# Layer 1's edge sums in two batches per group instead of four, and a reordered last group, in a two-layer graph attention kernel

## The chip, the cores and the metric

The kernel runs on one core of a Trainium2 chip. The metric is the device time of one execution in microseconds. Three executions of the kernel before took 2071.87, 2076.14 and 2081.02 us; their median is 2076.14 us. One more execution was recorded by the hardware profiler; it took 2070.48 us, and all views of the profile are of that one.

The engines are called PE (TensorE, matrix products; PEld is its loading of weights), DVE (VectorE), ACT (ScalarE), POOL (GpSimd) and SP (SyncE). Each works through its own queue of instructions strictly in the order in which the program lists them, and waits for the others by semaphores.

## The reference

A graph has 3125 nodes with 768 features and 53125 edges, sorted by the node they go to. Each edge has one of three relations. Two layers of relational graph attention are followed by a residual and a layer norm:

```python
def rgat_conv(x, W, q, k, b, src, dst, etype, heads, out_ch, n_nodes):
    xr = jnp.einsum('nd,rdf->rnf', x, W)
    oi = xr[etype, dst]
    oj = xr[etype, src]
    alpha = jax.nn.leaky_relu(oi @ q + oj @ k, NEG_SLOPE)
    m = jax.ops.segment_max(alpha, dst, num_segments=n_nodes)
    e = jnp.exp(alpha - m[dst])
    z = jax.ops.segment_sum(e, dst, num_segments=n_nodes)
    a = e / (z[dst] + EPS)
    msg = (a[:, :, None] * oj.reshape(-1, heads, out_ch)).reshape(-1, heads * out_ch)
    return jax.ops.segment_sum(msg, dst, num_segments=n_nodes) + b

h = jax.nn.elu(rgat_conv(x, W1, q1, k1, b1, ..., HEADS1, OUT1, n))   # 4 heads of 192
out = rgat_conv(h, W2, q2, k2, b2, ..., HEADS2, OUT2, n)             # 1 head of 768
return _layernorm(x + out, axis=-1)
```

So each layer has a dense part (every node's row times three 768 x 768 matrices) and an edge part (for every edge the row of its source under its relation is fetched, weighted, and added up at its target).

## The kernel before

**Groups, slots, rounds.** The sorted nodes are cut into NB = 25 groups of up to 128 nodes. A group's edges lie in SL = 17 slots of 128 edges each (the first group has SLF = 14). Since the edges are sorted, a slot's targets lie in one or two of the four 32-node windows of its group; `WINDOW` lists them. `ROUNDS` puts the slots into seven rounds such that the slots of one round have different windows: rounds 0 to 2 have three slots each, rounds 3 to 6 two. A slot's turn is its place when the rounds are read one after another.

**Three phases.** Phase 1 makes layer 1's table of rows for every node and relation, and the attention weights of layer 1's edges. Phase 2 (707 to about 1480 us of the profile) does two things woven together: the edge sums of layer 1 for one group, and the dense part of layer 2 for the group before it. Phase 3 does the edge part of layer 2, the residual and the layer norm. The order of the instructions is written out by hand: each phase is a loop over steps k, and lists of events tell which function is called at which step. No planner decides anything.

**Phase 2, in its steps.** At step k `gather(k)` has POOL fetch the rows of slot number k by an indirect DMA into one of 14 buffers (the nine `share` tiles and five `g` tiles); a buffer is free again when the sums of the slot 14 places earlier have read it. `high(k - 3)` has DVE write the slot's weight matrices `selp` (four heads, 32 or 64 columns; one tensor_scalar each, L857), into a pool of 9 buffers. `sums(k - 5)` (L861) issues PE's products of weights and rows (L878). Each has 32 output rows, one window, so products of one round that go to different windows lie in different quarters of the array. The sums don't go out slot by slot: `sums` returns without doing anything until a round is complete that closes a batch, and then issues all rounds of the batch, round by round and within a round head by head. The batches are rounds 0 and 1, 2 and 3, 4 and 5, and 6 alone; the last turns of these are the 6th, 11th, 15th and 17th slot of a group.

After a group's last sums come `e_y` (DVE divides by the weights' sum and adds the bias; L884 to L891), `e_x` (ACT's exponential, L897), `e_h` (DVE, L901 and L902), three steps after `e_y` `e_t` (PE's six transposes, L909), then `e_s` (ACT's copy of the result into `hT`, its high half, L916) and `e_s2` (DVE's difference, its low half, L922). From the sixth step after `e_y` on, `d_part` is called 18 times over 17 steps: six products of 128 x 128 weights each (L934; three per feature tile: high times wH, high times wL, low times wH), three calls for one half of one relation's rows. `d_row` copies each half out of `po` by ACT (L942), and SP stores finished rows into layer 2's table (L948). The last quarters of layer 2's weights for relation 2 are loaded by ACT's DMA queue at steps 14, 19, 23 and 26.

In a middle group PE's order is therefore: six transposes, 6 dense products, rounds 0 and 1, 36 dense products, rounds 2 and 3, 24 dense, rounds 4 and 5, 12 dense, round 6, 30 dense, and the next transposes.

**Phase 3, its end.** For each group: DVE's two scans (L1089, L1091) give the maxima, L1094 the exponents, `a_exp` (ACT, L1098) the exponential, `a_back` (PE, L1102) turns it, `a_put` (DVE, L1107) copies it to `p`, `high` (L1115) and `sums` (L1129) follow. Then `e_y`, `e_n` (mean and variance, L1172 to L1176), `e_sd` (ACT's square root, L1180), `e_low` (DVE's reciprocal and product, L1185 and L1187), `e_out` (ACT's scaling, L1192, and the store). Exponential and root need different function tables in ACT; the build puts an ACT_TABLE_LOAD ahead of each activation whose table isn't the one in place. In the steps of the loop `e_sd` of one group comes one step ahead of `a_exp` of the next, and `e_low` two steps ahead of `a_put`.

Of the kernel before, what the change touches and what calls it, by code (L numbers as in the profile page):

```python
# [8 lines left out]
F32 = mybir.dt.float32  # L9
# [4 lines left out]
AF = mybir.ActivationFunctionType  # L14
# [6 lines left out]
P = 128  # L21
# [16 lines left out]
SL = 17  # L38
# [8 lines left out]
          (3,), (3,), (3,))  # L47

ROUNDS = ((0, 7, 15), (1, 8, 16), (2, 9, 14), (3, 11), (4, 12), (5, 13), (6, 10))


@with_exitstack
def kernel(
# [23 lines left out]
    NB = (N + P - 1) // P  # L77
# [4 lines left out]
    H1 = l1["H"]  # L82
# [9 lines left out]
    V, S, G, T = nc.vector, nc.scalar, nc.gpsimd, nc.tensor  # L92
# [352 lines left out]
    def base(b):  # L445

        return SLF + (b - 1) * SL if b else 0

    def slots(b):
        return SL if b else SLF  # L450
# [5 lines left out]
    def rounds(b):  # L456
        return [[j for j in r if j < slots(b)] for r in ROUNDS]

# [370 lines left out]
    def phase2(work, psum, wH, wL):  # L829
# [13 lines left out]
        def in_turn(k):  # L843

            b, i = slot(k)
            return b, [j for r in rounds(b) for j in r][i]
# [4 lines left out]
        def high(k):  # L851

            b, j = in_turn(k)
            lo, hi = WINDOW[j][0] * 32, WINDOW[j][-1] * 32 + 32
            sel = work.tile([P, H1, 64], F32, name="selp", bufs=9)
            for h in range(H1):
                V.tensor_scalar(sel[:, h, :hi - lo], row[:, lo:hi], dl[:, b, j:j + 1], pall[:, b, j, h:h + 1],  # L857
                                op0=ALU.is_equal, op1=ALU.mult)
            st[b, j] = sel, gs[k % NG]

        def sums(k):  # L861

            b, j = in_turn(k)
            n = [i for i, r in enumerate(rounds(b)) if r[-1] == j]
            if not n or n[0] % 2 == 0 and n[0] < len(ROUNDS) - 1:
                return
            if n[0] < 2:
                blk[b] = {"acc": psum.tile([P, 2, 512], F32, name="acc", bufs=2)}
            acc = blk[b]["acc"]
            o = [(i, t) for r in rounds(b) for i in r for t in WINDOW[i]]  # L870
            for m, h in ((m, h) for m in range(n[0] // 2 * 2, n[0] + 1) for h in range(H1)):
                c = slice(h % 2 * CW, (h % 2 + 1) * CW)
                for i, t in o:
                    if i not in rounds(b)[m]:
                        continue
                    u = [x for x, y in o if y == t]
                    sel, g = st[b, i]
                    T.matmul(acc[32 * t:32 * t + 32, h // 2, c], sel[:, h, 32 * (t - WINDOW[i][0]):][:, :32],  # L878
                             g[:, h * CW:(h + 1) * CW], start=(i == u[0] and h % 2 == 0), stop=(i == u[-1]),
                             skip_group_check=True)  # L880
# [94 lines left out]
        for k in range(max(ev) + 1):  # L975
            if k < NK:
                gather(k)
            if k in (14, 19, 23, 26, 28):
                next(last_w2, None)
            if 0 <= k - LAG < NK:  # L980
                sums(k - LAG)
            if k == first:
                e_y(order[0])
                e_x(order[0])
            if 0 <= k - LAG + 2 < NK:
                high(k - LAG + 2)
            for f, a in ev.get(k, []):
                f(*a)
            if k == NK + LAG:
                for b in range(len(xbs)):  # L990
                    x_load3(b)
# [6 lines left out]
    def phase3(work, psum):  # L998
# [179 lines left out]
        def e_sd(b):  # L1178
            sd = blk[b]["sd"]
            S.activation(sd, sd, AF.Sqrt)  # L1180

        def e_low(b):
            s = blk[b]
            sd = s["sd"]
            V.reciprocal(sd, sd)  # L1185
            s["low"] = work.tile([P, 1], F32, name="low", bufs=2)
            V.scalar_tensor_tensor(s["low"], s["mv"][:, 0:1], -1.0, sd, op0=ALU.mult, op1=ALU.mult)  # L1187
# [19 lines left out]
        def when(k, f, *a):  # L1207
            ev.setdefault(k, []).append((f, a))

        LAG = SL + 10  # L1210
        for b in range(NB):
            when(max(base(b) - 12, 0), a_load, b)
            q = base(b) - 4 if b > 1 else 2 + 12 * b
            for i in range(5):
                when(q + 2 * i, a_spread, b, i)
                when(q + 1 + 2 * i, a_spread2, b, i)
            for d, f in ((10, a_q), (11, a_q2), (12, a_q3)):
                when(q + d, f, b)
            e = base(b) + slots(b)
            for d, f in ((2, a_alpha), (3, a_turn), (4, a_scan), (5, a_exp), (6, a_back), (7, a_put)):  # L1220
                when(e + d, f, b)
            s = base(b) + LAG + max(slots(b) - SL, -1)
            for n in range(len(ROUNDS)):
                when(s + n - 2, high, b, n)
                when(s + n, sums, b, n)
            s += len(ROUNDS)
            if b + len(xbs) < NB:
                when(s + 30, x_load3, b + len(xbs))
            for d, f in ((0, e_y), (1, e_n), (4, e_sd), (5, e_low), (7, e_out)):
                when(s + d, f, b)  # L1230
        for k in range(max(ev) + 1):
            if k < NK:
                gather(k)
# [7 lines left out]
    with tc.manual_schedule():  # L1241
        with tc.tile_pool(name="share", bufs=1) as pool:
# [4 lines left out]
            with tc.tile_pool(name="wbuf", bufs=1) as wbuf:  # L1247
                wH = wbuf.tile([P, R * DT, D + 2], F32R, name="wH")
                wL = wbuf.tile([P, R * DT, D + 2], F32R, name="wL")
                with tc.tile_pool(name="pre", bufs=1) as pre:  # L1250
                    qq = pre.tile([P, NB, H1, R], F32, name="qq")
                    with tc.tile_pool(name="work0", bufs=1) as work, tc.tile_pool(
                        name="psum0", bufs=1, space=PSUM
# [20 lines left out]
                    with tc.tile_pool(name="work1", bufs=1) as work, tc.tile_pool(  # L1274
                        name="psum1", bufs=1, space=PSUM
# [4 lines left out]
            with tc.tile_pool(name="work3", bufs=1) as work, tc.tile_pool(name="psum3", bufs=1, space=PSUM) as psum:  # L1280
                phase3(work, psum)
# [538 lines left out]
```

## Time and profile before

| what | us |
|---|---|
| median of three executions | 2076.14 |
| the profiled execution, its time | 2070.48 |
| its span | 2068.7 |
| PE busy | 1770.4 (86%) |
| DVE busy | 1195.9 (58%) |
| POOL busy | 1328.1 (64%) |
| ACT busy | 375.8 (18%) |
| PE busy in the dense products of phase 2, L934 (weights wH; wL) | 496.2; 305.0 |
| PE busy in the sums of phase 2, L878 (rows in share; in g) | 190.6; 118.6 |

The span is the time from the first to the last recorded instruction; the execution's own time is 1.8 us longer. A line such as `L934 PE MATMUL po<-wH,hT 128*128 128x386` names the line of the kernel, the engine, the operation, the tile written and the tiles read, the part of the array used (contraction by output rows) and the shape streamed. Products overlap in PE, so their busy times must not be added up: starts are what tells the pace. A product with 32-bit operands in the sums appears as two rows. `[6.21 <-PE acc L878]` behind an instruction means that its engine had been idle for 6.21 us and that the product of L878 was the last thing it waited for.

### The profile page before, as it was taken

How to read it: one execution, taken by the hardware profiler on the slowest of the kernel's cores; microseconds unless marked ns; L12 is line 12 of the kernel's file. 1: busy time of each engine (PE TensorE's matmuls, PEld its weight loads, DVE VectorE, ACT ScalarE, POOL GpSimd, SP SyncE). 2: the span in 40 equal slices, each digit the busy share in tenths (PEclk: the TensorE clock that was granted, in tenths of full speed). 3: DMA queues.
4: the chain of work that ended last, by engine and by line, in shares of the span. 5: the costliest groups of instructions: out<-in, count | busy, mean ns of one | idle time of the engine just before them, and what ended most of it. 6: DMA issues, size and time to landing. Idle time of an engine off the chain costs nothing.

```text
span 2068.7 us, 41981 instructions
## 1 busy us (share of the span) xinstructions
PE 1770.4 (86%) x15027; PEld 1477.3 (71%) x15027; DVE 1195.9 (58%) x4159; ACT 375.8 (18%) x659; POOL 1328.1 (64%) x1326
## 2 busy tenths in 40 slices
PE   6979998999989689999999999999756766766764
PEld 5979998998979578888888888888623433433433
DVE  6534554454443576676666667666356566666564
ACT  5411221122211011111111111111102112112112
POOL 5247777777777765655555565553277777777772
PEclk9989999999999899999999999999877777787786
DMA  6555554545546797877877787785689999999993
GB/s 187 190 137 176 162 191 146 175 160 174 177 148 197 268 338 263 267 252 255 279 258 252 269 265 254 255 280 189 213 311 329 339 343 334 341 325 320 325 320 125
DMA packets 156845, 506.33 MB, mean 245 GB/s; under 512 B 43875, under 2 KB 57069, under 8 KB 156628
## 3 DMA queue, kind: packets, MB, share of 16 engines
q0 software_dynamic: 81904, 331.52, 48.5%
q1 hardware_dynamic: 64494, 156.04, 21.7%
q10 hardware_dynamic: 10230, 15.98, 2.3%
q8 instruction: 123, 2.02, 0.4%
q14 instruction: 94, 0.77, 0.1%
HBM read 412.55 MB, written 95.69 MB: 246 GB/s over the span
## 4 chain that ended last, share of the span: by engine, by line
PE 61%; issue 12%; POOL 11%; DMA 8%; DVE 7%; ACT 1%; POOLq 0%; SPq 0%; DVEq 0%; ACTq 0%
PE po L934 23%; PE acc L1129 12%; PE acc L878 11%; POOL kt L466 9%; PE po L702 8%; DMA wL<-w_d 1%; POOL G L466 1%; PE bank L285 1%; PE pt L263 1%; DMA kt<-kt,ridx 1%; DVE F L1089 1%; PE bc L1036 1%; DVE stats L1172 1%; PE po L399 1%; PE pt L909 1%
## 5 line engine op out<-in xcount | busy, mean ns | idle before, releaser
L934 PE MATMUL po<-wH,hT 128*128 128x386 f32 (+1 forms) x1800 | 496.2, 346 | 0.9 <-ACT hT L916 0.9
L466 POOL DMA_INDIRECT kt<-kt,ridx x374 | 395.5, 1058 | 115.7 <-issue 109.1
L702 PE MATMUL po<-wH,xT 128*128 128x384 f32 x1584 | 442.0, 349 | 8.1 <-ACT share L717 4.4
L466 POOL DMA_INDIRECT G<-ftab,ridx x374 | 373.9, 1000 | 114.0 <-issue 81.7
L857 DVE TENSOR_SCALAR selp<-frow,fdl,pall 128x32 f32<-128x32 f32 (+1 forms) x1688 | 380.4, 318 | 0.2 <-PE acc L878 0.2
L466 POOL DMA_INDIRECT share<-ftab,ridx x239 | 238.9, 999 | 177.7 <-PE acc L878 132.9
L934 PEld LDWEIGHTS po<-wH,hT 128*128 128x128 f32 x1800 | 329.7, 189 | 31.2 <-issue 29.5
L702 PEld LDWEIGHTS po<-wH,xT 128*128 128x128 f32 x1584 | 295.9, 192 | 13.8 <-ACT share L717 6.3
L934 PE MATMUL po<-wL,hT 128*128 128x386 f32 (+1 forms) x900 | 305.0, 339 | 0.3 <-DMA wL<-w_d 0.3
L1129 PE MATMUL acc<-G,selp 128*32 128x386 f32 x2488 | 299.5, 578 | 3.6 <-DVE selp L1115 2.1
L702 PE MATMUL po<-wL,xT 128*128 128x384 f32 x792 | 271.2, 342 | 0.0
L1129 PEld LDWEIGHTS acc<-G,selp 128*32 128x32 f32 x2488 | 185.6, 127 | 79.6 <-issue 46.6
L466 POOL DMA_INDIRECT g<-ftab,ridx x135 | 134.9, 999 | 113.3 <-PE acc L878 88.0
L878 PE MATMUL acc<-share,selp 128*32 128x193 f32 x3208 | 190.6, 331 | 5.1 <-DMA share<-ftab,rfirst 4.1
L942 ACT COPY r<-po 128x386 f32<-128x386 f32 (+1 forms) x150 | 72.3, 482 | 604.7 <-PE po L934 603.1
L934 PEld LDWEIGHTS po<-wL,hT 128*128 128x128 f32 x900 | 170.1, 189 | 0.6 <-DMA wL<-w_d 0.6
L878 PEld LDWEIGHTS acc<-share,selp 128*32 128x32 f32 x3208 | 122.8, 111 | 51.1 <-issue 15.4
L702 PEld LDWEIGHTS po<-wL,xT 128*128 128x128 f32 x792 | 152.3, 192 | 0.0
L1042 DVE TENSOR_SCALAR sT<-bc,cols 128x512 bf16<-128x512 f32 (+1 forms) x125 | 83.4, 667 | 100.4 <-PE bc L1036 100.1
L1115 DVE TENSOR_SCALAR selp<-row_p,fdl,p 128x32 f32<-128x32 f32 (+1 forms) x422 | 110.7, 320 | 47.7 <-PE acc L1129 46.8
L1036 PE MATMUL bc<-d,one 1*128 1x512 bf16 (+1 forms) x125 | 48.6, 388 | 85.0 <-DVE sT L1042 82.3
L878 PE MATMUL acc<-g,selp 128*32 128x193 f32 x1768 | 118.6, 329 | 1.9 <-DMA g<-ftab,rfirst 1.9
(244 smaller groups left out, 1857.1 us busy)
## 6 DMA issues: line engine op xcount, KB each, us to landing
ftab<-share SPq DMA_DIRECT2D x75, 386.0 KB
ftab<-r SPq DMA_DIRECT2D x75, 386.0 KB
share<-in_L_gnn_W_dram SPq DMA_DIRECT2D x36, 384.0 KB
w_d<-w2hl SPq DMA_DIRECT2D x18, 768.0 KB
sT<-dr_d SPq DMA_DIRECT2D x25, 544.0 KB
share<-in_x_dram SPq DMA_DIRECT2D x25, 384.0 KB
xb_d<-share SPq DMA_DIRECT2D x25, 384.0 KB
xr<-in_x_dram SPq DMA_DIRECT2D x23, 384.0 KB
```

Source lines behind the costliest of these rows:

```text
L263: T.transpose(pt[:, f, c * P:(c + 1) * P], a[:, (2 * i + f) * P:(2 * i + f + 1) * P], ident)
L285: T.matmul(to, a[:, 2 * i + f, :], t[:, f, :w], start=(n == 0), stop=(n == 2 * DT - 1))
L466: return G.indirect_dma_start(out=to, out_offset=None, in_=tab, in_offset=_index(i[:, j:j + 1]), bounds_check=NP * R - 1, oob_is_err=False)
L702: m = T.matmul(po[:, :HALF], xT[:, s, t, :], w[:, i, sl], start=(n == 0), stop=(n == 3 * DT - 1))
L857: V.tensor_scalar(sel[:, h, :hi - lo], row[:, lo:hi], dl[:, b, j:j + 1], pall[:, b, j, h:h + 1], op0=ALU.is_equal, op1=ALU.mult)
L878: T.matmul(acc[32 * t:32 * t + 32, h // 2, c], sel[:, h, 32 * (t - WINDOW[i][0]):][:, :32], g[:, h * CW:(h + 1) * CW], start=(i == u[0] an ...
L934: T.matmul(po[:, :wd], hT[:, k, t, :], w[:, r * DT + t, sl], start=(t == 0 and n == 0), stop=(t == DT - 1 and n == 2))
L942: S.copy(o[:, c * HW:c * HW + wd], po[:, :wd])
L1036: T.matmul(bc[:, :n], one, s["d"][:, 4 * i * P:4 * i * P + n], start=True, stop=True)
L1042: V.tensor_scalar(s["sT"][:, 4 * i * P:4 * i * P + n], bc[:, :n], cols[:, b:b + 1], None, op0=ALU.is_equal)
L1115: V.tensor_scalar(sel, row_p[:, lo:hi], dl[:, b, j:j + 1], p, op0=ALU.is_equal, op1=ALU.mult)
L1129: T.matmul(acc[32 * t:32 * t + 32, c, :HW], st[b, j][:, 32 * (t - WINDOW[j][0]):][:, :32], gs[:, (base(b) + j) % NG, c * HW:(c + 1) * HW], ...
```

## The change

`BATCHES` names two batches for the sums of phase 2: rounds 0, 1 and 2, and rounds 3 to 6. `sums` now issues at the 9th and the 17th slot of a group. The order of the products among themselves is the same. The pool of `selp` has 12 buffers instead of 9. PE's order in a middle group becomes: six transposes, 30 dense products, rounds 0 to 2, 48 dense products, rounds 3 to 6, 30 dense, and the next transposes.

In phase 3, for the group before the last (NB - 2), `e_sd`, `e_low` and `e_out` come two steps later, so that its root stands behind the last group's exponential in ACT's order; `e_low` stays ahead of the last group's `a_put` in DVE's order. A new function `e_ready` has ACT take the exponential of a single number (`spare`, set once by DVE) five steps ahead of the last group's exponential.

```diff
+BATCHES = ((0, 1, 2), (3, 4, 5, 6))
...
-            sel = work.tile([P, H1, 64], F32, name="selp", bufs=9)
+            sel = work.tile([P, H1, 64], F32, name="selp", bufs=12)
...
             n = [i for i, r in enumerate(rounds(b)) if r[-1] == j]
-            if not n or n[0] % 2 == 0 and n[0] < len(ROUNDS) - 1:
+            batch = [x for x in BATCHES if n and n[0] == x[-1]]
+            if not batch:
                 return
-            if n[0] < 2:
+            if batch[0][0] == 0:
                 blk[b] = {"acc": psum.tile([P, 2, 512], F32, name="acc", bufs=2)}
...
-            for m, h in ((m, h) for m in range(n[0] // 2 * 2, n[0] + 1) for h in range(H1)):
+            for m, h in ((m, h) for m in batch[0] for h in range(H1)):
...
+        spare = work.tile([1, 1], F32, name="spare", bufs=1)
+        V.memset(spare, 1.0)
+
+        def e_ready():
+
+            S.activation(spare, spare, AF.Exp)
...
             for d, f in ((0, e_y), (1, e_n), (4, e_sd), (5, e_low), (7, e_out)):
-                when(s + d, f, b)
+                when(s + d + (2 if b == NB - 2 and d > 1 else 0), f, b)
+        when(base(NB - 1) + SL, e_ready)
```

## The prediction

> **What bounds the kernel now.** I read the chain of work that ended last first, to see which engine the end hangs on; then the busy time of each engine by stretch; then, inside the stretch that the change touches, the instructions in order of time. The chain by line:
>
> ```profile
> PE po L934 23%; PE acc L1129 12%; PE acc L878 11%; POOL kt L466 9%; PE po L702 8%; DMA wL<-w_d 1%; POOL G L466 1%; PE bank L285 1%; PE pt L263 1%; DMA kt<-kt,ridx 1%; DVE F L1089 1%; PE bc L1036 1%; DVE stats L1172 1%; PE po L399 1%; PE pt L909 1%
> ```
>
> L934 (layer 2's dense products) and L878 (layer 1's sums) are 34% of the span, both TensorE in the middle phase, the one whose batches change. The table by stretch, with the columns stretch, length, busy time and instructions of PE, of its weight loads, of DVE, ACT and POOL, granted clock, DMA share, GB/s:
>
> ```profile
> 763.36:1458.35 694.99, 694.99 (x7224) 601.30 (x7222) 458.31 (x1932) 104.32 (x184) 376.77 (x377) 1.00 0.76 253
> 1540.00:2030.00 490.00, 333.65 (x2804) 195.93 (x2799) 300.87 (x893) 86.62 (x109) 375.60 (x376) 0.77 0.93 331
> ```
>
> From 763 to 1458 us PE is busy for all of it at full clock: what saves PE time there saves it at the end, as long as no new wait appears. The last phase is another world (DMA at 93%): apart from its last group the change leaves it alone. One period of the middle phase, PE in order of time (start, length of the merged row, line, tiles, count):
>
> ```profile
> 1058.22 0.34 PE L934 MATMUL po<-wL,hT 128*128 128x384 f32 x1
> 1058.40 0.34 PE L934 MATMUL po<-wH,hT 128*128 128x384 f32 x1
> 1058.67 1.51 PE L878 MATMUL acc<-share,selp 128*32 128x193 f32 x16
> 1060.11 0.44 PE L934 MATMUL po<-wH,hT 128*128 128x384 f32 x1
> 1060.39 0.34 PE L934 MATMUL po<-wL,hT 128*128 128x384 f32 x1
> ...
> 1065.51 0.82 PE L909 MATMUL pt<-fident,ey 128*128 128x128 f32 x6
> 1066.08 0.42 PE L934 MATMUL po<-wH,hT 128*128 128x384 f32 x1
> ...
> 1067.31 1.67 PE L878 MATMUL acc<-share,selp 128*32 128x193 f32 x33
> ...
> 1070.07 0.44 PE L934 MATMUL po<-wH,hT 128*128 128x384 f32 x1
> ```
>
> The reader is to see starts, not lengths: L934 runs at one start per 0.175 us, and each change between wide (128*128) and narrow (128*32) products breaks that step.
>
> **Part 1: fewer batches.** No product is added or removed; the sums keep their order and move between the dense parts. *What a batch costs beyond its products:* (a) into it, 1058.40 to 1058.67 is 0.27 where 0.175 is regular: 0.09. (b) out of it: round 6 alone (16 rows, 8 steps of two products side by side) takes 1058.67 to 1060.11, 1.44; rounds 0 and 1 (64 rows, 33 of them in the row shown; 16 steps of four) take 1067.31 to 1070.07, 2.76. Eight more steps cost 1.32, so 0.165 each, and 1.44 less eight of them leaves 0.12. (c) the first dense step after it, 1060.11 to 1060.39, is 0.28: 0.105 over. Together 0.31 us. Check: a period holds 108 dense products (108 x 0.175 = 18.9), 56 steps (9.24), 4 batches (1.24) and the transposes (0.65): 30.0, against 30.2 measured (1458.35 less 763.36, over 23 groups).
>
> Two batches fewer in a group are 0.62 us. Group 0 has no dense products between its sums and gains nothing. Groups 2 to 24 are 23: **-14.3 us**. Group 1 I count at nothing: there the dense part of relation 2 stands 0.49 us still at about 762, waiting for the last quarter of wL (issued 733.0, landed 762.3), and arriving 0.62 earlier may only lengthen that. If wL lands sooner because the gathers behind group 1's later first batch start some 3 us later, up to 0.62 + 0.49 more is gained. Bounds of part 1 without new waits: -14.3 to -15.4.
>
> *What is behind the moved batches.* Four things could take the gain back.
>
> (1) The dense products of the next group. Before, rounds 0 and 1 stood between the transposes L909 and the first product that reads the new hT. Now only two dense parts (12 products) do. Transposes at T = 1065.51; the first dense product 0.57 later, then 0.26 and eleven steps of 0.175: the new group's first product starts at T + 2.76, the third, which reads the low half, at T + 3.11, with its weights loaded from T + 2.94. The two halves come from
>
> ```profile
> 1066.36 0.80 ACT L916 CAST hT<-pt 128x768 fp32r<-128x768 f32 x1 [1.19 <-PE pt L909]
> 1067.19 0.96 DVE L922 TENSOR_TENSOR hT<-pt,hT 128x768 fp32r<-128x768 f32 x1 [0.24 <-ACT hT L916]
> ```
>
> High half done at T + 1.65, low half at T + 2.64, in all the groups from 2 on within 0.04. The cover shrinks from about 3 us to 0.3 and holds. ACT and DVE have the same work in the same order between the last batch's end and here (the last batch ends at the same step of the loop, with 30 dense products between it and L909 as before, and DVE is still 0.27 us ahead of them).
>
> (2) The gathers. POOL waits for the sums to free a buffer:
>
> ```profile
> 1069.08 0.99 POOL L466 DMA_INDIRECT share<-ftab,ridx  x1 [6.21 <-PE acc L878]
> 1070.38 1.00 POOL L466 DMA_INDIRECT share<-ftab,ridx  x1 [0.30 <-PE acc L878]
> ```
>
> The first comes 1.77 after the batch began (round 0's end), then one each 1.30. The landings in the trace are 5.4 us after the issue (median; 7.4 at most between 780 and 1430; 10.2 around 710, where weights load). With 14 buffers the slots 14, 15 and 16 of a group's turn take those of its round 0. Their gathers now leave 1.8, 3.1 and 4.4 us after the first batch starts and land by 11.8 at worst. The second batch starts 24 x 0.165 + 48 x 0.175 + 0.3 = 12.7 after the first, and round 6, which needs the last two, 4 us later: 16.7. About 5 us to spare, where there were some 11. Slots 6 to 8 of the next group wait for round 3 of the second batch and have 9. Seventeen gathers of 1.30 are 22 us of a period of 29.6, so POOL catches up.
>
> (3) The weights of the sums (selp). Twelve buffers let DVE run twelve slots ahead of the oldest unsummed one. Slots 12 to 16 need rounds 0 and 1 of the first batch; 20 tensor_scalars at 0.23 (row L857 has 64-wide ones of that step) are 4.6 us, in 12.7. The six slots behind the second batch fit too: DVE has to be through 8 of these (1.8 us) after L922, at T + 4.5, and the first batch starts at about T + 6.0.
>
> (4) The acc, po and row buffers: group ends keep their places, so acc is released as before; ACT's copies of 0.48 us fit in any dense run. I cost (2) to (4) at zero; each us that one missed would cost 23 us, since nothing else on PE stands by.
>
> **Part 2: the last group of the last phase.**
>
> ```profile
> 2041.09 0.28 DVE L1094 TENSOR_TENSOR e<-pa,B 17x128 f32<-17x128 f32 x1
> ...
> 2041.45 1.28 ACT L1098 ACT_TABLE_LOAD   x1 [2.07 <-DVE sd L1185]
> 2042.74 0.31 ACT L1098 ACTIVATE e<-e 17x128 f32<-17x128 f32 x1
> ...
> 2043.42 0.18 DVE L1107 COPY p<-pa 128x17 f32<-128x17 f32 x1 [1.79 <-PE pa L1102]
> ...
> 2058.23 1.28 ACT L1180 ACT_TABLE_LOAD   x1 [14.26 <-DVE sd L1176]
> 2059.52 0.20 ACT L1180 ACTIVATE sd<-sd 128x1 f32<-128x1 f32 x1
> ```
>
> Everything here is on the path. In the built program ACT's order at the end becomes: the new small exponential, group 24's exponential, a table load, group 23's root, group 23's output, group 24's root. Both loads shown are gone; one is new, behind group 24's exponential. The small exponential finds its table already in place and costs ACT about 0.2 us while it is idle; its memset is one short DVE instruction at the phase's start.
>
> The end gains the load at 2058.23: -1.29. The load at 2041.45 gains nothing by itself, because DVE's order is kept: group 23's reciprocal and its stt (L1185, L1187) stand ahead of the copy of group 24's weights (L1107), with group 24's 17 selp and all its sums behind. The reciprocal waits for the root, and that now comes after the new load: exponential at 2041.42, its 0.31, the load 1.28, root 2043.02 + 0.20, reciprocal 2043.26, stt 2043.46, copy 2043.65. It was 2043.42: **+0.23**, carried through the PE-bound sums to the end. Sum **-1.06**.
>
> Here the Trainium skill weighs in (ScalarE: Activation LUTs, What ACT_TABLE_LOAD costs): it gives about 1.28 us for the load and a drain of about 1.38 beside it at each change of set. The rows show no drain: the activation starts 0.01 us after the load. But ACT was idle ahead of each load here, and the new one follows an activation directly. With that drain only there, the copy comes 1.61 late and part 2 is -1.29 + 1.61 = +0.3. I take the row; +0.3 stays as the end of the range, and -1.4 (root's load hidden altogether, nothing late) as the other.
>
> **Sum.** -14.3 - 1.06 = -15.4. Profiled execution: 2070.48 (span 2068.7) to 2055.1. That execution lies 5.7 below the median of the three times shown (2076.14, spread 2071.87 to 2081.02); the forecast is for the median: **2060.8**, 0.74% less.
>
> **The rivals.**
> *Half the price.* (a) to (c) may not be per batch: a longer batch may end dearer, or dense products be slowed when they run 48 in a row. For it: rounds of different width have never run back to back for more than 16 steps. Against: step and price are equal, to 0.01, in batches of 8 and 16 steps over all groups. Half is -7.2 - 1.1: 2068.
> *The hT cover is too thin* ((1) above). If L922 slips behind one more slot of selp (four tensor_scalars, 0.92 us), PE stands 0.6 us in each group, which is the whole gain: 2075. Against: DVE's order there is unchanged, and it waits 0.24 for ACT, not ACT for it.
> *Slower: gathers in bursts.* They come 9 and 8 at a time instead of at most 6; 9 x 395 KB (128 rows of 3088 bytes) in 11.7 us is 304 GB/s beside the row stores, where this stretch had 253 on the mean. It decides once a landing takes more than 12.3 us (16.7 - 4.4): each us above it costs 23, so at 13.5 us it is +28 against -15.4: 2088. For it: 10.2 was seen around 710. Against: the burst's early gathers are the ones needed first, and the last phase moves 331.
> *It does nothing*, because PE is not the bound: the table says it is.
>
> **How the numbers follow.** Likeliest case 76%, 2060.8, its own range 2054 to 2066 (the spread of a median, the wL term, the table load). Half price 11%, 2068; thin hT cover 6%, 2075; gathers 7%, 2080 to 2095. A range of 2053 to 2070 leaves out the last two and little else. About 0.5% (10.4 us, 2065.8) can be told from no change. Faster: nearly all of the first case and a little of the second, 0.77; same: the rest of these and the thin cover, 0.15; slower: 0.08.
>
> **What would show it.** Right: PE busy through the middle phase with two narrow runs of 96 and 104 rows a group, a period of 29.6 us, the same 0.27, 0.12 and 0.28 at each change; POOL idle in one long piece a group, waits on acc; at the end two table loads fewer and one new, L1107's copy 0.2 later against the scan, the last root without a load. Wrong: idle PE ahead of the first product that reads a new hT, or inside a narrow run with a gather as its releaser; a period over 30; an end more than 1.5 us from the sum.

## The result, and the profile after

| | us |
|---|---|
| before, median of 6 runs | 2077.51 (2071.87 to 2081.42) |
| after, median of 6 runs | 2056.76 (2054.32 to 2059.23) |
| ratio | 0.9901, 95% [0.9883, 0.9919] |
| after, the profiled execution (its span) | 2056.61 (2054.8) |

The change is 20.7 us faster (16.8 to 24.3 by the interval), the time is inside the predicted range and 4 us below the predicted value. Of the runs below, e9 and e10 fell where every kernel was slower (the kernel before 2666.76 us, at a granted clock of 0.83 to 0.84 instead of 0.91 to 0.92), and they are compared with that one alone.

First the chain of work that ended last, by line, of the kernel after:

```profile
PE po L937 24%; PE acc L881 11%; PE acc L1132 11%; POOL kt L468 9%; PE po L704 6%; DMA G<-ftab,ridx 2%; POOL G L468 2%; DMA kt<-kt,ridx 2%; PE bank L287 1%; PE pt L265 1%; PE pt L912 1%; DVE F L1092 1%; PE po L401 1%; PE bc L1039 1%; DVE stats L1175 1%
```

L937 is the dense product (L934 before), L881 layer 1's sums (L878 before). One line is gone from the front of it: the load of wL, which had 1% before. Then the busy times by stretch, the same two lengths as shown of before:

```profile
747.20:1442.19 694.99, 694.99 (x7370) 618.11 (x7369) 464.38 (x1969) 106.62 (x188) 388.16 (x388) 1.00 0.77 262
1523.84:2013.84 490.00, 332.55 (x2778) 195.41 (x2773) 299.61 (x889) 86.71 (x110) 375.64 (x376) 0.77 0.93 330
```

PE is still busy for the whole of the middle phase, and does 7370 products in the time of 7224 before. The last phase is what it was. One period of the middle phase, PE in order of time:

```profile
1032.91 0.34 PE L937 MATMUL po<-wH,hT 128*128 128x386 f32 x1
1033.18 2.98 PE L881 MATMUL acc<-share,selp 128*32 128x193 f32 x65
...
1037.27 0.44 PE L937 MATMUL po<-wH,hT 128*128 128x384 f32 x1
1037.55 0.34 PE L937 MATMUL po<-wL,hT 128*128 128x384 f32 x1
...
1045.67 0.34 PE L937 MATMUL po<-wH,hT 128*128 128x384 f32 x1
1045.94 1.67 PE L881 MATMUL acc<-g,selp 128*32 128x193 f32 x34
...
1051.33 0.44 PE L937 MATMUL po<-wH,hT 128*128 128x384 f32 x1
1051.61 0.34 PE L937 MATMUL po<-wL,hT 128*128 128x384 f32 x1
...
1056.56 0.34 PE L937 MATMUL po<-wH,hT 128*128 128x384 f32 x1
1056.77 0.84 PE L912 MATMUL pt<-fident,ey 128*128 128x128 f32 x6
1057.37 0.42 PE L937 MATMUL po<-wH,hT 128*128 128x384 f32 x1
```

Two narrow runs a group: 96 rows from 1033.18 to 1037.27 (4.09 us; 24 steps of 0.165 and 0.12 are 4.08) and 104 rows from 1045.94 to 1051.33 (5.39; 32 steps, not all of them four products wide, and 0.12 are 5.40). The way in is 0.27 and the first dense step after a run 0.28, as before. New is the last dense product to the transposes, 1056.56 to 1056.77: 0.21 here, 0.21 to 0.25 in most groups, where it was 0.18 (1065.33 to 1065.51 before).

The period, from the transposes of group 1 to those of group 24 over 23, went from 30.217 to 29.647 us. Where the 13.9 us between the two spans lie, by the starts of marked instructions in the two traces:

| stretch | before | after | difference |
|---|---|---|---|
| to group 0's transposes | 731.02 | 729.09 | -1.9 |
| group 0's to group 1's transposes | 32.34 | 31.21 | -1.1 |
| 23 groups of the middle phase | 694.99 | 681.89 | -13.1 |
| group 24's transposes to the last gather of phase 3 | 575.81 | 576.29 | +0.5 |
| last gather to the last group's division by its sum (L1168) | 21.49 | 24.46 | +3.0 |
| from there to the end | 13.04 | 11.89 | -1.2 |

The first, fourth and fifth rows hold nothing that the change touches but the late copy of part 2 (0.17): over the executions of e1 to e5, e7, e8, e11 and e12 below the first alone goes from 727.0 to 735.4, and without e8 the fifth from 21.4 to 23.9, whatever the batches. The medians lie further apart than these two executions, because the profiled one of before was 7 us under its median and that of after at it.

### The profile page after: what moved, and what is told of

Its sections match the earlier page's. It is cut to its first block, busy times and chain, and to the rows that moved or that the text cites. A ratio compares the mean times of both kernels' runs of the same rounds, so it can differ in the third digit from the quotient of the medians.

```text
span 2054.8 us, 41907 instructions
## 1 busy us (share of the span) xinstructions
PE 1757.6 (86%) x15027; PEld 1485.2 (72%) x15027; DVE 1192.5 (58%) x4160; ACT 373.9 (18%) x658; POOL 1329.0 (65%) x1326
## 4 chain that ended last, share of the span: by engine, by line
PE 58%; issue 13%; POOL 12%; DMA 8%; DVE 6%; ACT 1%; POOLq 0%; SPq 0%; DVEq 0%; ACTq 0%
PE po L937 24%; PE acc L881 11%; PE acc L1132 11%; POOL kt L468 9%; PE po L704 6%; DMA G<-ftab,ridx 2%; POOL G L468 2%; DMA kt<-kt,ridx 2%; PE bank L287 1%; PE pt L265 1%; PE pt L912 1%; DVE F L1092 1%; PE po L401 1%; PE bc L1039 1%; DVE stats L1175 1%
## 5 line engine op out<-in xcount | busy, mean ns | idle before, releaser
L937 PE MATMUL po<-wH,hT 128*128 128x386 f32 (+1 forms) x1800 | 483.8, 343 | 0.9 <-ACT hT L919 0.9
L937 PEld LDWEIGHTS po<-wH,hT 128*128 128x128 f32 x1800 | 329.5, 189 | 16.5 <-issue 14.7
L937 PE MATMUL po<-wL,hT 128*128 128x386 f32 (+1 forms) x900 | 304.9, 339 | 0.0
L881 PE MATMUL acc<-share,selp 128*32 128x193 f32 x3208 | 186.0, 330 | 4.6 <-DMA share<-ftab,rfirst 2.5
L937 PEld LDWEIGHTS po<-wL,hT 128*128 128x128 f32 x900 | 170.3, 189 | 0.0
L881 PEld LDWEIGHTS acc<-share,selp 128*32 128x32 f32 x3208 | 125.8, 111 | 45.8 <-issue 7.4
L719 ACT COPY share<-po 128x384 f32<-128x384 f32 x144 | 67.9, 478 | 275.5 <-PE po L704 272.2
```

What stands on the lines that cost most here:

```text
L719: S.copy(to, po[:, :HALF].rearrange("p (h f) -> p h f", h=2))
L937: T.matmul(po[:, :wd], hT[:, k, t, :], w[:, r * DT + t, sl], start=(t == 0 and n == 0), stop=(t == DT - 1 and n == 2))
```

## The experiments

Each was timed in turn with the kernel before on the same chip; "before" is that run's own.

**e1: the kernel before against itself.** No edit.

> The kernel before, unchanged. My theory: the 20.7 us between the medians are some 15 us of mechanism and some 5 us of spread, because the profiled execution of before (2070.48) lay below all its timed ones; then the unchanged kernel shows no difference from itself (within 0.2%), single executions from 2070 to 2082, and a second profile differs from the first in phases 1 and 3, with the middle phase at 30.2 us a group again. Rival (the missing 5 us are a real effect of the change): executions all within 2 us of the median, and the same split over the phases in both profiles.

2073.49 (2068.84 to 2078.21) against 2077.06 (2068.72 to 2084.51): 0.9988 [0.9972, 1.0004]. What this method calls a difference starts at some 3 us; and single times of this kernel spread over 16 us (29 executions) and over 9 (the 12 of e1), those of after over 8 (11 executions).

**e2: part 1 alone, e3: part 2 alone.** e2 takes the end of phase 3 back, e3 the batches:

```diff
e2
-        spare = work.tile([1, 1], F32, name="spare", bufs=1)
...
-                when(s + d + (2 if b == NB - 2 and d > 1 else 0), f, b)
-        when(base(NB - 1) + SL, e_ready)
+                when(s + d, f, b)
e3
-BATCHES = ((0, 1, 2), (3, 4, 5, 6))
...
-            sel = work.tile([P, H1, 64], F32, name="selp", bufs=12)
+            sel = work.tile([P, H1, 64], F32, name="selp", bufs=9)
...
-            for m, h in ((m, h) for m in batch[0] for h in range(H1)):
+            for m, h in ((m, h) for m in range(n[0] // 2 * 2, n[0] + 1) for h in range(H1)):
```

> Part 1 alone: two batches and 12 selp buffers, phase 3 as before. Theory: the middle phase at 29.65 us a group as in the full change, and 13 to 19 us less than before, all of the gain but about 1 us. Rival (the tail is worth the missing 5 us): 14 us less and no more, the rest in the run with part 2 alone.

> Part 2 alone: four batches as before, only the last group's order in phase 3 changed. Theory: 1 us less (a table load of 1.28 gone at the last root, the copy of the last group's weights 0.2 later), which the times cannot tell from nothing; the last root without a load in the trace. Rival: 5 us less or more.

e2: 2057.39, ratio 0.9911 [0.9885, 0.9936], 29.650 us a group. e3: 2076.9, ratio 1.0 [0.9983, 1.0017], 30.22 a group (median). So the batches carry the whole measured gain, and part 2 is too small for a median. It can be read in the trace: from the last group's variance (L1179) to its root takes 1.53 us before and in e2, 0.25 in after and e3 (-1.28); from the last group's exponents to the copy of its weights 2.33 before and in e2, 2.50 in after and e3 (+0.17).

The end of phase 3 of the kernel after, ACT and then DVE in order of time:

```profile
2028.01 0.31 ACT L1101 ACTIVATE e<-e 17x128 f32<-17x128 f32 x1 [18.77 <-DVE e L1097]
2028.34 1.28 ACT L1183 ACT_TABLE_LOAD   x1
2029.63 0.20 ACT L1183 ACTIVATE sd<-sd 128x1 f32<-128x1 f32 x1
...
2045.54 0.20 ACT L1183 ACTIVATE sd<-sd 128x1 f32<-128x1 f32 x1 [14.25 <-DVE sd L1179]
```

```profile
2027.64 0.28 DVE L1097 TENSOR_TENSOR e<-pa,B 17x128 f32<-17x128 f32 x1
2029.87 0.16 DVE L1195 RECIPROCAL sd<-sd 128x1 f32<-128x1 f32 x1 [1.95 <-ACT sd L1183]
2030.07 0.16 DVE L1197 SCALAR_TENSOR_TENSOR low<-mv,sd 128x1 f32<-128x1 f32 x1
2030.14 0.17 DVE L1110 COPY p<-pa 128x17 f32<-128x17 f32 x1
```

The load follows the exponential 0.33 us after that began, and the exponential takes 0.31: there is no drain between them, nor before the root (0.01). The reciprocal's wait of 1.95 is the late copy's cause, and the last root has no load ahead of it.

e3's profile shows something else. PE in order of time around the start of group 1's second half, in e3:

```profile
763.46 0.52 PE L934 MATMUL po<-wH,hT 128*128 128x386 f32 x2
...
769.29 0.69 PE L934 MATMUL po<-wL,hT 128*128 128x384 f32 x1 [5.31 <-DMA wL<-w_d]
769.77 0.84 PE L934 MATMUL po<-wH,hT 128*128 128x384 f32 x2
```

PE stands 5.31 us for the last quarter of wL. In the profiled execution of before it stood idle for 0.32 (0.49 by starts), in e1 not at all:

```profile
761.54 0.52 PE L934 MATMUL po<-wH,hT 128*128 128x386 f32 x2
762.38 0.44 PE L934 MATMUL po<-wL,hT 128*128 128x384 f32 x1 [0.32 <-DMA wL<-w_d]
```

Behind the pause of e3 the products start 0.32 apart for a while instead of 0.175 (769.77 to 770.41 is two steps). Group 0's to group 1's transposes take 39.27 in e3, 32.58 in e1: these 6.7 us are the largest part of the 10.6 by which the span of e3, 2077.6, is longer than that of e1 (another 4.3 lie ahead of group 0's transposes, where the two kernels are the same). This is the term that the prediction counts at nothing.

**e4: three batches.** Rounds 2 and 3 apart, the rest as after:

```diff
-BATCHES = ((0, 1, 2), (3, 4, 5, 6))
+BATCHES = ((0, 1), (2, 3), (4, 5, 6))
```

> The full change with three batches, rounds 0 and 1, 2 and 3, 4 to 6. Theory (a fixed price for each batch): 29.9 us a group, half way between 30.2 and 29.65, and 7 to 10 us less than before. Rival (the gain comes from the 12 selp buffers or from gathers in larger bursts, not from the number of changes): a group at 29.65 or at 30.2.

2066.16 against 2077.06 (-10.9), ratio 0.9954 [0.9938, 0.997], that is -9.6 us (-6.2 to -12.9); 30.002 us a group, 0.215 less than with four. The transposes stand late here too: 0.22 to 0.25 behind the last dense product in most groups, where before has 0.18, and the first of them is 0.03 longer, so one batch fewer saves 0.30 and 0.08 of it goes to a wait. 23 x 0.215 and part 2's 1.1 make 6.0, at the near end of the interval.

**e5: group 1 alone in two batches.** All other groups in four, group 0 too; part 2 and the twelve selp buffers as in after.

```diff
-BATCHES = ((0, 1, 2), (3, 4, 5, 6))
+BATCHES = ((0, 1), (2, 3), (4, 5), (6,))
+FIRST = ((0, 1, 2), (3, 4, 5, 6))
...
-            batch = [x for x in BATCHES if n and n[0] == x[-1]]
+            batch = [x for x in (FIRST if b == 1 else BATCHES) if n and n[0] == x[-1]]
```

> The full change, but only group 1 (and group 0, where nothing stands between the sums) in two batches; groups 2 to 24 keep four. Theory (the last quarter of wL lands sooner because the later first batch of group 1 holds the gathers back): the last quarter lands some 20 us after its issue, as in both profiles with two batches, not 29 to 35 as in the profiles with four, PE never waits for it, the groups from 2 on take 30.2, and the time is 1.5 to 6 us less than before. Rival (the early landing has another cause, the clock or chance): the quarter lands 29 us or more after its issue.

2071.41 against 2075.51: 0.9979 [0.9963, 0.9996], that is -4.1 us (-0.8 to -7.7), of which part 2 is 1.1. The period of the other groups is 30.219, that of before, so the twelve buffers alone gain nothing. By the medians one group's change is worth about 3 us, where two batches' price is 0.62; but the interval, less part 2, reaches from a gain of 6.6 to a loss of 0.3. What else differs is when the last quarter of wL lands. The time from its issue to the end of its last packet, and PE's idle time for it, in the profiled executions (PE went on some 0.5 us after that packet where it waited):

| group 1 in | kernel | landed after | PE then waited |
|---|---|---|---|
| four, three or seven batches | before, e1, e4 | 28.9, 28.8, 28.6 | 0.32, 0, 0 |
| | e7 | 30.8 | 2.4 |
| | e3 | 35.0 | 5.3 |
| two batches | after, e2, e5, e8 | 18.8, 21.3, 23.8, 20.3 | 0 |
| | e11, e12 | 11.6, 14.5 | 0 |

With two batches POOL's gathers stand for their buffers for 5.9 to 12.3 us in one piece near the issue, with more batches the longest such pause in the 25 us behind it is 1.5 to 3.4; the DMA engines are over 90% busy around it, and the load lands sooner. e10 below, with four batches, has a pause of 9.83 and a landing after 9.9: the early landing goes with the pause, not with the number of batches as such. The last quarter in after (ACT's queue) and the pause (POOL), then the pause of before:

```profile
731.08 3.44 ACTq L520 DMA_DIRECT2D wL<-w_d  x1
739.52 1.01 POOL L468 DMA_INDIRECT share<-ftab,rfirst  x1 [6.59 <-PE acc L881]
```

```profile
738.23 1.00 POOL L466 DMA_INDIRECT share<-ftab,rfirst  x1 [3.37 <-PE acc L878]
```

**e6: nine buffers for the gathered rows instead of fourteen.** This kernel computes something else: its loop names the gather nine slots ahead before the sums that still read the buffer, so the sums take other slots' rows.

```diff
-        gs = share + [work.tile([P, RW], F32, name=f"g{i}", bufs=1) for i in range(5)]
+        gs = share[:]
```

> The full change with 9 gather buffers instead of 14. Eight of a group's gathers then wait for the first batch and the last one leaves 10.9 us after it starts, where round 6 needs it 16.7 after. Theory (landing takes 5.4, 7.4 at most): PE waits 0 to 1.6 us in a group, a group at 29.7 to 31.2, the time 0 to 36 us over the full change, and with 14 buffers some 5 us are to spare. Rival (bursts of gathers land much later): a group at 33 or more.

2242.12, ratio 1.0789 [1.0761, 1.0816], 37.1 us a group. With its dependences turned round it says nothing of the gathers' slack; e11 asks the question properly.

**e7: seven batches.** Each round by itself:

```diff
-BATCHES = ((0, 1, 2), (3, 4, 5, 6))
+BATCHES = ((0,), (1,), (2,), (3,), (4,), (5,), (6,))
```

> The full change with seven batches, one for each round. Theory (0.31 us for each batch, whatever its length): three batches more than before, 31.1 us a group, 21 us over the kernel before, up to 28 if the last quarter of wL lands later still. Rival (a short batch is cheaper than a long one, or the price is paid once for a group): 30.3 to 30.6 us a group.

2097.08, ratio 1.0095 [1.007, 1.012], 21.6 us over the before of 2075.51 (14.5 to 24.9 by the interval). The median period is 31.21, so three batches more than before cost 0.33 each; 23 x 0.99 less part 2's 1.1 is 21.7. One of its narrow runs, PE in order of time (rows of one run overlap and are merged):

```profile
833.58 0.34 PE L937 MATMUL po<-wH,hT 128*128 128x384 f32 x1
833.84 0.36 PE L881 MATMUL acc<-g,selp 128*32 128x193 f32 x3
...
835.30 0.44 PE L937 MATMUL po<-wH,hT 128*128 128x384 f32 x1
835.58 0.34 PE L937 MATMUL po<-wL,hT 128*128 128x384 f32 x1
```

In 0.26, eight steps and the way out 1.46, first dense step 0.28: the price per change is the same for a run of 8 steps, of 16 and of 32.

**e8: DVE's work ahead of the transposes one step earlier, and the root of the group before the last behind the copy of the last group's weights.** On top of after:

```diff
-                for d, f in ((0, e_y), (1, e_x), (2, e_h), (3, e_t), (4, e_s), (4, e_s2)):
+                for d, f in ((0, e_y), (1, e_x), (1, e_h), (3, e_t), (4, e_s), (4, e_s2)):
...
-                when(s + d + (2 if b == NB - 2 and d > 1 else 0), f, b)
+                when(s + d + ({4: 2, 5: 4, 7: 2}.get(d, 0) if b == NB - 2 else 0), f, b)
```

> The full change and two repairs. First, DVE's two instructions of e_h one step earlier, ahead of four selp, so that they end 0.9 us earlier before the transposes: theory, the 0.05 us that PE now waits there goes, a group at 29.60 instead of 29.65, 1 us in all. Second, in the last phase group 23's e_low two steps later than in the change, behind the copy of group 24's weights and its first three selp: theory, that copy comes about 1.1 us after the exponents instead of 2.5, and 1.4 us are gained. Sum 2.4 us under the full change, which the times can hardly tell; the trace can. Rival (the new places only move the wait): both distances unchanged.

2052.13 (2049.7 to 2055.32), ratio 0.9887 [0.9864, 0.991] to a before of 2075.51; span 2048.4. It is the shortest of all; its interval overlaps that of after, the trace tells them apart. The period is 29.576, the transposes come 0.177 behind the last dense product. DVE in order of time in e8, first ahead of a group's transposes (these start at 848.23), then at the end:

```profile
845.68 0.56 DVE L904 TENSOR_SCALAR ey<-ey 128x768 f32<-128x768 f32 x1
846.28 0.96 DVE L905 SCALAR_TENSOR_TENSOR ey<-y,ey 128x768 f32<-128x768 f32 x1
...
2022.72 0.28 DVE L1097 TENSOR_TENSOR e<-pa,B 17x128 f32<-17x128 f32 x1
2023.77 0.18 DVE L1110 COPY p<-pa 128x17 f32<-128x17 f32 x1 [0.78 <-PE pa L1105]
2023.99 0.78 DVE L1118 TENSOR_SCALAR selp<-row_p,fdl,p 128x32 f32<-128x32 f32 x3
2024.94 0.17 DVE L1195 RECIPROCAL sd<-sd 128x1 f32<-128x1 f32 x1 [0.18 <-ACT sd L1183]
```

DVE is done at 847.24, 1.0 us ahead of the transposes. At the end the copy comes 1.05 us after the exponents began, where after has 2.50 and before 2.33, and the reciprocal no longer stands ahead of it. Both of after's leftovers are gone: 0.07 x 23 = 1.6 us and 1.4 us.

**e9, e10, e11, e12: nine buffers with the gathers named in time.** e9 and e11 are one kernel: after with nine buffers for the gathered rows, the gather of a slot named five slots later than in after, so that it waits for the sums that use its buffer. e10 is the kernel before, e12 the kernel after.

```diff
-        gs = share + [work.tile([P, RW], F32, name=f"g{i}", bufs=1) for i in range(5)]
+        gs = share[:]
...
-            if k < NK:
-                gather(k)
+            if 0 <= k - 5 < NK:
+                gather(k - 5)
```

> The full change with 9 gather buffers instead of 14 and each gather named five steps later in the loop, so that it stands behind the sums whose buffer it takes (in the run with nine buffers before this one it stood ahead of them, and the sums read other slots' rows). The last gather of a group leaves 10.9 us after the first batch starts; round 6 needs it 16.7 after. Theory (landing takes 5.4 us, 7.4 at most): PE waits 0 to 1.6 us a group, 29.7 to 31.2 us a group, 0 to 36 us over the full change; with 14 buffers some 5 us are to spare. Rival (bursts land much later): a group at 33 or more.

> The kernel before once more, for a third profile of its start. Theory (with four batches the gathers of group 1 and 2 keep the weights waiting): the last quarter of wL lands 28 us or more after its issue and PE waits between 0 and 6 us for it. Rival: it lands 18 to 24 us after, as in the profiles with two batches.

> The kernel with nine gather buffers and late gathers once more, since the call before found the chip slow for every kernel (the kernel before at 2667 us). Theory as there: 29.7 to 31.2 us a group, 0 to 36 us over the full change. Rival: 33 or more a group.

> The full change once more, beside the one with nine buffers. Theory: 29.65 us a group, the last quarter of wL landed 18 to 24 us after its issue and no wait of PE for it, single executions within 6 us of one another, 16 to 23 us under the kernel before. Rival (the gain above 15.4 us was chance): 15 us or less under it, or a wait for wL as in one profile with four batches.

e9 took 2750.76 against a before of 2666.76, ratio 1.031 [1.0273, 1.0347], and 39.1 us a group against 35.2 in e10 (medians), whose one execution took 2663.26. The kernel after was not run beside them, so what part of e9's 84 us the buffers have is not known. In e10 the last quarter of wL landed 9.9 us after its issue, where 28 or more was expected; POOL stood 9.83 us for a buffer around that issue. e11: 2068.3, ratio 0.996 [0.9946, 0.9975]. e12: 2057.81, ratio 0.9907 [0.9888, 0.9926]; its last quarter landed after 14.5 us, sooner than the 18 to 24 expected. With five buffers less the kernel is 10.5 us slower than after; its period is 30.16 (median) instead of 29.65. In e11, first the sums as a group of instructions over the middle phase (their busy time, mean ns of one, and PE's idle time ahead of them with what ended it), then one long run of PE in order of time:

```profile
L881 PE MATMUL acc<-share,selp 128*32 128x193 f32 x4296 | 213.6, 328 | 3.3 <-DMA share<-ftab,ridx 3.0
```

```profile
843.23 0.33 PE L937 MATMUL po<-wH,hT 128*128 128x384 f32 x1
843.50 6.08 PE L881 MATMUL acc<-share,selp 128*32 128x193 f32 x104
849.50 0.45 PE L937 MATMUL po<-wH,hT 128*128 128x384 f32 x1
```

The run of 104 rows takes 6.00 there, 5.39 to 6.52 over the groups and 5.93 on the mean, where it is 5.39 in after, and what PE waits for are gathers. These 0.54 x 23 are 12.5 us, less what the transposes gain, which are prompt again in most groups; idle time alone, 3.3 us, shows only a part of it. In after the same groups of instructions over the same stretch have no idle time ahead of them:

```profile
L881 PE MATMUL acc<-share,selp 128*32 128x193 f32 x2824 | 161.2, 328 | 0.0
L881 PE MATMUL acc<-g,selp 128*32 128x193 f32 x1576 | 103.3, 328 | 0.0
```

So fourteen buffers hold the gathers' bursts off PE, and nine do not. A batch structure needs the buffers that go with it.

## Why the prediction was right, point by point

**(a), (b), (c), the price of a batch: right.** Predicted 0.31 us. Measured: 0.33 (e7, three more), and from the periods of e8 (two fewer, no new wait) 30.217 - 29.576 = 0.64, 0.32 each. The parts are the same 0.27, 0.12 and 0.28 in before, after, e7 and e8. The rival of half the price falls: a run of 32 steps costs no more to leave than one of 8, and 48 dense products in a row keep 0.175.

**The period: predicted 29.6, measured 29.647.** Each group lost some 0.08 of its two batches' 0.64 to a wait that the prediction says is not there. The step that failed is in (1): "ACT and DVE have the same work in the same order [...] DVE is still 0.27 us ahead". The order is the same, but one instruction is longer. L904 (L901 before), DVE, all middle groups, first before and then after; the columns are the durations in ns, least, median and most:

```profile
L901 DVE TENSOR_SCALAR ey<-ey x23: 546/552/718, 791.8 to 1455.8; 128x768 f32<-128x768 f32 x23
```

```profile
L904 DVE TENSOR_SCALAR ey<-ey x23: 551/725/737, 788.1 to 1439.6; 128x768 f32<-128x768 f32 x23
```

The 0.17 us come where a gather is being issued by POOL. DVE in two groups of after, and POOL at the same times:

```profile
995.71 0.72 DVE L904 TENSOR_SCALAR ey<-ey 128x768 f32<-128x768 f32 x1
...
1025.32 0.55 DVE L904 TENSOR_SCALAR ey<-ey 128x768 f32<-128x768 f32 x1
1025.91 0.96 DVE L905 SCALAR_TENSOR_TENSOR ey<-y,ey 128x768 f32<-128x768 f32 x1
```

```profile
995.04 1.00 POOL L468 DMA_INDIRECT g<-ftab,ridx  x1 [0.30 <-issue]
...
1024.83 1.16 POOL L468 DMA_INDIRECT g<-ftab,ridx  x1 [0.30 <-issue]
1026.30 1.44 POOL L468 DMA_INDIRECT g<-ftab,ridx  x1 [0.30 <-PE po L937]
```

At 995.71 DVE takes 0.72 under a gather of 1.00; at 1025.32 DVE takes its usual 0.55 and the gather 1.16. In before POOL had run out of free buffers by then: its wait of 6.21 us for the next batch lay over this instruction (1062.87 to 1069.08 over 1063.68). After the change a second batch of four rounds frees a burst of buffers, and POOL is still issuing. So DVE ends 0.15 ahead of the transposes instead of 0.27, which is less than PE needs: the last dense step is 0.22 instead of 0.18 (medians) and the first transpose 0.03 longer. In the group at 1025.32 the step is the old 0.18 (1026.97 to 1027.15). The diff touches neither instruction. The pairing holds over all groups behind the first in eleven traces (all but e6, e9 and e10): 94 of these instructions took 0.71 to 0.75, and each of them began 0.65 to 0.68 us after a gather did; the 121 with no gather beside them took 0.55 to 0.56. In before one group has it as well (0.72 at 1214.75), and there too the step is 0.218. e8, which starts L904 a step earlier, has 0.56 there and the step back at 0.177. The link from POOL's burst to PE's wait is shown by this pairing and by e8's cure; a run that moves only the gathers was not made.

**(1), the cover of hT: right.** High half done at T + 1.68 and low half at T + 2.67 (predicted 1.65 and 2.64), the new group's first product at about T + 2.8, no idle time ahead of it. The thin-cover rival falls, by the 0.3 us that the low half has to spare.

**(2), the gathers: right, with the margin that was said.** Landings of 5.3 us (median) and 7.5 at most, as before (5.4, 7.4); the worst case of 12.3 that the rival needed was not met. e11 shows that the cover is real: with five buffers less the wait appears. One sign was read wrong: POOL's idle time does not fall in one long piece a group but in two (mostly 6.8 and 1.4), as it did before (mostly 6.2 and 1.8), the second batch having a wait of its own.

**(3), (4): nothing was seen of either.** No idle time ahead of the sums (the two rows above) or of the dense products over 22 groups.

**Part 2: -1.28 + 0.17 = -1.1, predicted -1.29 + 0.23 = -1.06.** The row was the right one to take: the load was in no way dearer behind an activation than behind an idle ACT, and the drain of about 1.38 that the Trainium skill gives (ScalarE: Activation LUTs, What ACT_TABLE_LOAD costs) does not show in the two places where it could.

**The sum, and what was mis-sized.** Of the -15.4, the traces give 23 x 0.57 = -13.1 and -1.1, which is -14.2, 1.2 short: the wait at the transposes took 1.6 (what e8 gets back), and the price, 0.32 instead of 0.31, gave 0.5. Group 1, "at nothing" with "up to 0.62 + 0.49 more", came 1.1 sooner in this pair of traces (the table's second row), just that upper end. But the measured -20.7 is 5.3 more than predicted, and this excess is explained only in part. The term that looks too small is group 1: e5 puts it at about -3 (all of e5, -4.1 [-0.8, -7.7], less part 2's 1.1), with an interval that reaches past zero. The prediction looked at the wL wait of one execution, 0.49 us. It is a wait that differs from run to run, 0 to 5.3 us in the five executions of e5's table with more batches, and absent in the six with two. A gain that lies in how often a wait happens is not in one profile. It is not the whole spread of the times: those of e5, whose profile has no such wait, still lie 11.8 us apart, and the stretch to group 0's transposes, which no run changes, takes from 727.0 to 735.4. 13.1 + 1.1 + 3 is 17.2; the remaining 3.5 of the median are inside the interval (-16.8 to -24.3; e12 has -18.7, e2 without part 2 has -18.5 by its ratio), and are left open. Against the weights as the whole answer stands e4: its group 1 is not in two batches, its load landed as late as before's, and it too is 3.6 better than its steps (-9.6 against 6.0), though inside its interval.

The step from the profiled execution to the median failed with it: it carried the 5.7 us, by which before's profiled execution lay under its median, over to after, whose own lies at its median (2056.61 to 2056.76).

## What to carry to other kernels

Where one engine is the bound, count the changes of shape in its order and read the price of one from starts in the trace; it added up the same for 8, 16 and 32 steps, so fewer, longer runs are worth exactly that, as long as the buffers grow with them. A change of order on one engine also changes which other engines are busy at the same time: look at what two engines that share something do at the moment of the tightest margin, and move the victim a step earlier. A wait for a transfer that lands late once differs from execution to execution: read it in several, since a change that removes it may gain more than one profile says.

## What the runs showed of the hardware that was not expected

- A DVE tensor_scalar of 128 x 768 in fp32 takes 0.55 us, and 0.71 to 0.75 where it began 0.65 to 0.68 us after a gather that POOL was issuing; the gather then took 1.00. Where DVE kept its 0.55 the gather took longer: 1.16 in after, where it began 0.49 ahead of DVE, and 1.34 to 1.39 in most groups of e8, where it began 0.04 to 0.09 behind. The scalar_tensor_tensor behind it, with two operands from SBUF, took 0.96 in every one of the 25 groups, gather or not. The Trainium skill (GPSIMD Engine Reference, Specifications) names a contention of the two engines for SBUF for DVE's two-port mode and for two operands from SBUF. The rows show none at the instruction with two operands; that the tensor_scalar ran in the two-port mode no run here shows.
- A load of 1152 KB on ACT's queue landed after 11.6 to 35.0 us in the same place of eleven executions: 11.6 to 23.8 where POOL's gathers paused for 5.9 us or more in one piece near the issue, 28.6 to 35.0 where the longest pause in the 25 us behind it was 3.4.
- After PE's pause of 5.31 us in e3 its products started at 0.32 instead of 0.175; the granted clock was 0.79 over the ten us from 770, and 1.00 in before over the 13 us from 762, whose pause was 0.32.
